# Fixed turn for score banks, one bank for side work, denominators in pairs by transfers and GpSimd, mask kept in memory: one core, masked attention with three layer norms

## The chip, the cores and the metric

The kernel runs on one core of a Trainium2 chip. The metric is device time in microseconds (us), and lower is better. "Slower" or "faster" means a difference of over 2%. TensorE is PE in the profile, VectorE is DVE, ScalarE is ACT, GpSimd is POOL, SyncE is SP.

## The reference, cut to what matters

```python
# x: (F=8, N=2048, C=256) float32; adj: (2048, 2048) int32, about 0.8% ones; H=8 heads, D=32
q, k, v = split(x @ w_qkv)                       # per frame f
scores  = einsum('fnhd,fmhd->fhnm', q, k) / sqrt(D)
attn    = softmax(where(adj > 0, scores, -1e9))
t       = einsum('fhnm,fmhd->fnhd', attn, v)
y       = layernorm(x + t, g1, b1)
z       = layernorm(y + relu(y @ w1 + b1_) @ w2 + b2_, g2, b2)
out     = layernorm(x + z)
```

## The kernel before

A block is 128 keys by 512 queries by four heads. Sixteen blocks are a group (one half of the heads), two groups a chunk of 512 queries, four chunks a frame. For each block PE makes scores into two score tiles (two PSUM banks each), DVE adds the mask while it empties them into a P buffer, ACT takes the exponential in place, and PE multiplies by the values. Two blocks of scores are made ahead.

The softmax denominators are sums of the P buffers over the keys. Seven of sixteen blocks go to PE one by one as products with ones ("lone terms"). Five are added up by GpSimd, four by accumulating transfers, and each of the two sums is one more term:

```python
pp   = pool(bufs=6)                     # P buffers, 1 MB each
ps_s = pool(bufs=3, PSUM)               # three score tiles, also used by all side work
ps_o, ps_d = pool(bufs=1, PSUM), pool(bufs=1, PSUM)     # values' sum, denominator
mask = mkp.tile([P, MB, N], F8)         # the whole mask, on chip
POOLED = (0, 1, 4, 7, 10)
MOVED = (2, 5, 8, 11)
ALONE = [m for m in range(MB) if m not in POOLED + MOVED]
# values(item), after the four value matmuls of block mb:
    if mb == POOLED[1]:
        nc.gpsimd.tensor_tensor(ACC[grp], PT.pop((f, qc, g, POOLED[0])), PT.pop(item), ALU.add)
    elif mb in POOLED[2:]:
        nc.gpsimd.tensor_tensor(ACC[grp], ACC[grp], PT.pop(item), ALU.add)
    elif mb in MOVED[1:]:
        nc.gpsimd.dma_start(PT[f, qc, g, MOVED[0]], PT.pop(item), accum_op=ALU.add)
    terms = [PT.pop(item)] if mb in ALONE else []
    if mb == LAST:
        terms += [ACC.pop(grp), PT.pop((f, qc, g, MOVED[0]))]
    for n, term in enumerate(terms):    # four matmuls each into the denominator's bank
        ...
```

Beside the blocks runs side work, a piece a block: the tail of the chunk before (division, residual, three norms, two layers of the MLP, about 20 blocks long), in the last chunk of a frame the projections of the next frame, and in frame 0 the turning of the mask.

## Time and profile before

| | before |
|---|---|
| time | 4264.85 us median of 3 (4258.01 to 4278.54) |
| profiled run | span 4279.2 us, granted clock 0.954 |
| PE / DVE / ACT / POOL busy | 90 / 66 / 57 / 44% |
| DVE idle in front of a masking, behind scores | 920 us |
| time at half clock, from the clock's records | 392 us |

The prediction shows rows of the page and works out from them what bounds the kernel. Three rows of DVE's waits (columns: us in total, times, longest us):

```profile
DVE p L146 <- PE s L143: 920.2, 676, 24.6
DVE p L146 <- DMA p<-p: 96.9, 59, 3.3
DVE RS L219 <- PE s L217: 100.2, 32, 7.1
```

The second row is DVE waiting for a P buffer that a transfer still reads, the third is the reciprocals waiting for the turned denominators.

### The profile page before, as it was taken

The numbers are of one execution on the slowest core, as the hardware profiler recorded it, in microseconds if no ns is written. First come the engines' busy times: TensorE is split into PE (matmuls) and PEld (weight loads), VectorE is DVE, ScalarE is ACT, GpSimd is POOL, SyncE is SP. The second block draws the span as 40 slices with busy tenths as digits, with TensorE's granted clock in tenths as the row PEclk, the third lists the DMA queues.
The fourth block names the chain that finished last, engine by engine and source line by source line (L and its number), as shares of the span: only waits on it lengthen the run. The fifth ranks groups of instructions, "written<-read, shape, count | busy, mean of one in ns | idle before, by whom it ended". The sixth has DMA issues, their size and how long they took to land. (4 is left out here: it accounts for less than half of the span.)

```text
span 4279.2 us, 57066 instructions
## 1 busy us (share of the span) xinstructions
PE 3863.4 (90%) x24068; PEld 1267.8 (30%) x24068; DVE 2814.4 (66%) x3175; ACT 2439.0 (57%) x1809; POOL 1896.5 (44%) x841
## 2 busy tenths in 40 slices
PE   7988989999999989999899998999989999899996
PEld 3222232222322223222232223322233222332222
DVE  2766747777477765777557775577756777467774
ACT  3655645555466655666555655556655565556564
POOL 1444425545245543545435444355533554344453
PEclk9988999999999999999999999999999999999998
DMA  3342323222233221233223223223231323222222
GB/s 108 73 105 63 69 69 65 55 60 60 60 70 69 60 69 40 60 70 70 69 41 66 62 60 78 41 60 69 61 77 33 69 60 70 69 49 60 60 60 54
DMA packets 89654, 274.13 MB, mean 64 GB/s; under 512 B 6064, under 2 KB 56368, under 8 KB 64816
## 3 DMA queue, kind: packets, MB, share of 16 engines
q0 software_dynamic: 27648, 201.34, 23.4%
q1 hardware_dynamic: 61744, 69.09, 5.2%
q8 instruction: 190, 3.11, 0.3%
q14 instruction: 72, 0.59, 0.0%
HBM read 52.30 MB, written 16.78 MB: 16 GB/s over the span
## 5 line engine op out<-in xcount | busy, mean ns | idle before, releaser
L146 DVE TENSOR_TENSOR p<-s,mask 128x1024 f32<-128x1024 f32 x2048 | 2407.8, 1217 | 1102.6 <-PE s L143 920.2
L148 ACT ACTIVATE p<-p 128x2048 f32<-128x2048 f32 x1024 | 1956.1, 1910 | 1586.5 <-DVE p L146 1264.3
L143 PE MATMUL s<-qT,kT 32*128 32x512 f32 x8192 | 1552.3, 658 | 177.9 <-DVE p L146 164.5
L172 POOL TENSOR_TENSOR acc<-acc,p 128x2048 f32<-128x2048 f32 x192 | 872.7, 4545 | 682.8 <-ACT p L148 525.3
L166 PE MATMUL o<-p,v 128*32 128x512 f32 x8192 | 1137.4, 628 | 35.1 <-ACT oT L185 34.1
L143 PEld LDWEIGHTS s<-qT,kT 32*128 32x128 f32 x8192 | 473.5, 187 | 1119.6 <-DVE p L146 555.7
L181 PE MATMUL den<-p,ones 128*32 128x512 f32 x4096 | 561.3, 621 | 0.0
L170 POOL TENSOR_TENSOR acc<-p 128x2048 f32<-128x2048 f32 x64 | 291.5, 4554 | 474.9 <-ACT p L148 277.6
L166 PEld LDWEIGHTS o<-p,v 128*32 128x32 f32 x8192 | 163.2, 109 | 847.3 <-issue 574.3
L232 POOL TENSOR_TENSOR y<-y,in 128x1024 f32<-128x1024 f32 x32 | 75.4, 2355 | 553.3 <-DVE y L229 553.3
L117 PE MATMUL s<-turned,wqkv 128*128 128x512 f32 x512 | 239.6, 613 | 12.6 <-ACT turned L111 12.6
L181 PEld LDWEIGHTS den<-p,ones 128*32 128x32 f32 x4096 | 140.1, 116 | 341.9 <-issue 340.6
L205 ACT ACTIVATE y<-y,nb,rs 128x256 f32<-128x256 f32 x384 | 198.3, 588 | 45.3 <-DVE nb L203 45.3
L194 DVE BATCH_NORM_STATS2 st<-y 128x6 f32<-128x256 f32 x384 | 154.3, 402 | 73.3 <-POOL y L273 70.9
L197 POOL TENSOR_SCALAR rs<-mv 128x4 f32<-128x4 f32 x96 | 18.2, 190 | 380.4 <-DVE mv L195 377.6
L174 POOL DMA_DIRECT2D p<-p x192 | 170.6, 888 | 27.9 <-ACT p L148 23.5
L117 PEld LDWEIGHTS s<-turned,wqkv 128*128 128x128 f32 x512 | 93.8, 192 | 161.2 <-issue 129.4
L271 POOL TENSOR_TENSOR y<-y,g2r 128x1024 f32<-128x1024 f32 x32 | 76.0, 2376 | 124.3 <-ACT y L205 124.3
L254 PE MATMUL s<-turned,w1s 128*128 128x512 f32 x256 | 121.2, 617 | 3.0 <-ACT turned L246 3.0
L243 PE MATMUL s<-ident,y 128*128 128x128 f32 x256 | 66.0, 349 | 64.0 <-ACT y L205 63.5
L248 POOL TENSOR_TENSOR y<-y,g1r 128x1024 f32<-128x1024 f32 x32 | 75.3, 2352 | 103.3 <-PE s L243 99.8
L264 PE MATMUL s<-w2s,hT 128*128 128x256 f32 x512 | 119.2, 386 | 0.8 <-ACT hT L257 0.8
(55 smaller groups left out, 1683.4 us busy)
## 6 DMA issues: line engine op xcount, KB each, us to landing
p<-p POOLq DMA_DIRECT2D x192, 1024.0 KB, 7.0
in<-in_x_dram SPq DMA_DIRECT2D x64, 512.0 KB, 6.5
in<-in_adj_dram SPq DMA_DIRECT2D x32, 512.0 KB, 5.1
out_dram<-y SPq DMA_DIRECT2D x32, 512.0 KB, 3.3
wqkv<-in_L_gnn_w_qkv_dram SPq DMA_DIRECT2D x1, 768.0 KB, 4.3
w1s<-in_L_gnn_w_dram SPq DMA_DIRECT2D x1, 256.0 KB, 4.5
w2s<-in_L_gnn_w_dram SPq DMA_DIRECT2D x1, 256.0 KB, 4.8
g1r<-in_L_gnn_ln_g_dram SPq DMA_DIRECT2D x1, 128.0 KB, 4.8
```

The lines of the kernel that those rows point to most:

```text
L117: nc.tensor.matmul(ps[:, g, :], wqkv[:, a, k0 + g * P:k0 + (g + 1) * P], xT[:, a, :], start=(a == 0), stop=(a == 1))
L143: nc.tensor.matmul(ps2[half][:, j, :], KT[f, mb // TPC][r:r + D, g, (mb % TPC) * P:(mb % TPC + 1) * P], QT[f, qc][r:r + D, g, :], start=Tr ...
L146: nc.vector.tensor_tensor(pt[:, 2 * half:2 * half + 2, :], ps, mask[:, mb, qc * CH:(qc + 1) * CH][:, None, :].to_broadcast([P, 2, CH]), AL ...
L148: nc.scalar.activation(pt, pt, AF.Exp, scale=1.0 / math.sqrt(D))
L166: nc.tensor.matmul(O[grp][r:r + D, :], V[f, mb // TPC][:, mb % TPC, g * P + r:g * P + r + D], pt[:, h, :], start=(mb == 0), stop=(mb == LAST))
L170: nc.gpsimd.tensor_tensor(ACC[grp], PT.pop((f, qc, g, POOLED[0])), PT.pop(item), ALU.add)
L172: nc.gpsimd.tensor_tensor(ACC[grp], ACC[grp], PT.pop(item), ALU.add)
L174: nc.gpsimd.dma_start(PT[f, qc, g, MOVED[0]], PT.pop(item), accum_op=ALU.add)
L181: nc.tensor.matmul(DEN[grp][r:r + D, :], cst["ones"], term[:, h, :], start=(mb == ALONE[0]), stop=(n == 2))
L194: nc.vector.bn_stats(st, t[:, j, :])
L205: nc.scalar.activation(t[:, j, :], t[:, j, :], AF.Identity, bias=nb[:, j:j + 1], scale=rs[:, j:j + 1])
L254: nc.tensor.matmul(ph[:, d, :], w1s[:, a, d * P:(d + 1) * P], yT[:, a, :], start=(a == 0), stop=(a == 1))
```

## The change

The intent was to take work and waits away from PE and the score banks. Seven pairs of a group are added by accumulating transfers, GpSimd adds up the pairs, and PE gets three terms a group instead of nine, five blocks into the next group. Side work leaves the score tiles: it gets whichever of two single banks the values' sum doesn't use, so the score tiles keep a fixed turn. All of it is cut into smaller pieces, with set numbers of blocks between them. The mask goes to DRAM and 512 queries of it are loaded at a time. The room that this frees makes nine P buffers of six. The residuals come by accumulating transfers straight into y. There is one y buffer.

```diff
-    pp = ctx.enter_context(tc.tile_pool(name="pp", bufs=6))
+    pp = ctx.enter_context(tc.tile_pool(name="pp", bufs=9))
-    ps_s = ctx.enter_context(tc.tile_pool(name="ps_s", bufs=3, space=bass.MemoryType.PSUM))
-    ps_o = ctx.enter_context(tc.tile_pool(name="ps_o", bufs=1, space=bass.MemoryType.PSUM))
-    ps_d = ctx.enter_context(tc.tile_pool(name="ps_d", bufs=1, space=bass.MemoryType.PSUM))
+    ps_s = [ctx.enter_context(tc.tile_pool(name=f"ps_s{i}", bufs=1, space=bass.MemoryType.PSUM)) for i in range(3)]
+    ps_x = [ctx.enter_context(tc.tile_pool(name=f"ps_x{i}", bufs=1, space=bass.MemoryType.PSUM)) for i in range(2)]
... (project, turn_mask, tail: each piece takes one bank() and yields the blocks to wait)
-    POOLED = (0, 1, 4, 7, 10)
-    MOVED = (2, 5, 8, 11)
-    ALONE = [m for m in range(MB) if m not in POOLED + MOVED]
+    NPAIR = MB // 2 - 1
+    ISSUE, ADD, SUM = 2, 5, 20
+    def denominators(t):
+        ...
+        item = block(ISSUE)
+        f, qc, g, mb = item
+        if mb % 2 == 0 and mb // 2 < NPAIR:
+            nc.gpsimd.dma_start(PT[f, qc, g, mb + 1], PT.pop(item), accum_op=ALU.add)
+        f, qc, g, mb = block(ADD)
+        grp, k = (f, qc, g), mb // 2
+        if mb % 2 == 0 and 0 < k < NPAIR:
+            pair = PT.pop((f, qc, g, mb + 1))
+            if k == 1:
+                ACC[grp] = ap.tile([P, 4, CH], F32, name="acc")
+                nc.gpsimd.tensor_tensor(ACC[grp], PT.pop((f, qc, g, 1)), pair, ALU.add)
+            else:
+                nc.gpsimd.tensor_tensor(ACC[grp], ACC[grp], pair, ALU.add)
... (tail)
-        nc.gpsimd.tensor_tensor(y, y, xs, ALU.add)
+        nc.gpsimd.dma_start(y, xin, accum_op=ALU.add)
...
             while (nf, nmb // TPC) not in V:      # a block whose projection isn't made yet
-                advance()
+                advance(t0)                       # runs side work, whatever is first in line
+                t0 += 1
```

## The prediction

> **What bounds the kernel now.** I first read the busy row and the groups of the page. A "block" here is 128 keys by 512 queries by four heads; there are 1024, in 64 groups of 16, two groups to a chunk of 512 queries, 32 chunks.
>
> ```profile
> PE 3863.4 (90%) x24068; PEld 1267.8 (30%) x24068; DVE 2814.4 (66%) x3175; ACT 2439.0 (57%) x1809; POOL 1896.5 (44%) x841
> L146 DVE TENSOR_TENSOR p<-s,mask 128x1024 f32<-128x1024 f32 x2048 | 2407.8, 1217 | 1102.6 <-PE s L143 920.2
> L172 POOL TENSOR_TENSOR acc<-acc,p 128x2048 f32<-128x2048 f32 x192 | 872.7, 4545 | 682.8 <-ACT p L148 525.3
> L181 PE MATMUL den<-p,ones 128*32 128x512 f32 x4096 | 561.3, 621 | 0.0
> L174 POOL DMA_DIRECT2D p<-p x192 | 170.6, 888 | 27.9 <-ACT p L148 23.5
> p<-p POOLq DMA_DIRECT2D x192, 1024.0 KB, 7.0
> ```
>
> PE at 90% looks like the bound, but a matmul that waits for its bank counts as busy. So I went to the timeline of a quiet stretch:
>
> ```profile
> 1999.63 2.36 DVE L146 TENSOR_TENSOR p<-s,mask 128x1024 f32<-128x1024 f32 x2 [0.17 <-PE s L143]
> 2000.44 1.60 PE L143 MATMUL s<-qT,kT 32*128 32x512 f32 x8
> 2001.97 1.07 PE L166 MATMUL o<-p,v 128*32 128x512 f32 x8
> 2002.16 2.36 DVE L146 TENSOR_TENSOR p<-s,mask 128x1024 f32<-128x1024 f32 x2 [0.17 <-PE s L143]
> 2002.85 1.04 PE L181 MATMUL den<-p,ones 128*32 128x512 f32 x8
> 2003.83 1.14 PE L143 MATMUL s<-qT,kT 32*128 32x512 f32 x8
> ```
>
> Two DVE starts lie 2.53 us apart: the first half of the masking frees a bank (1.2), the scores refill it (1.14), about 0.2 of signalling. The scores row shows 1.60 there and 1.14 when nothing is waited for. PE's own work in a plain block is about 2.05 us (scores 1.07 and values 0.97, start to start), so it has 0.48 us of slack; a denominator term of 0.97 us makes the block 2.95, which is 0.42 more. This is a DVE-PE loop and not a full PE.
>
> The starts of the exponentials, read from the timeline, give the chunks: 116.5 us for an ordinary one (1794.94 to 1911.43), 159.7 where the next frame is projected (2064.00 to 2223.70), some 140 for the second and third of frame 0, where masks are turned. 32 plain blocks would take 81.0. The other 35.5 us of an ordinary chunk are, by my reading of the periods: 14 denominator terms at 0.42, 5.9; the two ends of groups, 9.2; the tail (both norms, the MLP, the last norm), about 20.
>
> The tail's long steps are seen here:
>
> ```profile
> 1820.20 0.33 PE L243 MATMUL s<-ident,y 128*128 128x128 f32 x1 [1.52 <-ACT y L205]
> 1825.17 2.36 DVE L146 TENSOR_TENSOR p<-s,mask 128x1024 f32<-128x1024 f32 x2 [4.07 <-PE s L143]
> 1828.00 3.70 PE L254 MATMUL s<-turned,w1s 128*128 128x512 f32 x8
> 1832.91 2.36 DVE L146 TENSOR_TENSOR p<-s,mask 128x1024 f32<-128x1024 f32 x2 [5.38 <-PE s L143]
> 1820.00:1824.00 4.00, 3.60 (x16) 1.95 (x16) 1.10 (x1) 4.00 (x7) 0.83 (x1) 0.57 1.03 209
> 1824.00:1828.00 4.00, 4.00 (x25) 0.60 (x17) 2.36 (x2) 1.14 (x3) 3.92 (x3) 0.58 0.28 57
> ```
>
> DVE sits idle for 4 to 5 us behind one piece of side work on PE. The last two rows are windows (length, busy of PE, PEld, DVE, ACT, POOL, granted clock, DMA): after PE's 1.5 us wait the clock is 0.57 for 8 us.
>
> **What the skill says.** "SBUF — State Buffer", section "SBUF: two separate sides": GpSimd and a VectorE operation with two SBUF inputs take the shared ports as an exclusive lock, for the whole instruction. The trace agrees: the small nb (both inputs in SBUF) takes 151 ns free and a median of 1274, at most 4264, and those over 1 us that I looked at end some 20 ns after a GpSimd addition. The masking reads one operand from PSUM and keeps 1217 ns beside GpSimd or not. "TensorE: Matmul & The Clock Gate", section "What's actually happening", has the array fall to half clock after an idle window; the windows above agree in kind. "DMA: Bandwidth & Descriptors", section "Anatomy of one DMA — SWDGE (gpsimd) path", gives about 2.0 us plus bytes over 436 GB/s, an estimate of 4.4 us for 1 MB. This trace has 7.0 for the accumulating transfer, which I use.
>
> **The change part by part.**
>
> Denominators. Nine terms a group become three: seven pairs are added by transfers, GpSimd sums the seven, and PE takes the sum and the last two blocks, five blocks into the next group. PE busy falls by two thirds of 637 us (561.3 and 76.2 for the acc form), 425 us, but most of that lay in slack. On the path, before: 5.9 + 9.2 = 15.1 us a chunk. After: two steps of 3 x 0.97 = 2.9, less slack 0.48, so 2.4 each, and about 0.5 each for turning and the reciprocal: 5.9. Saving 9.2 a chunk.
>
> Banks. Side work no longer takes a score bank, so the turn of three pairs is kept and a score waits for one half of a masking. Before, a step with side work shifted the turn, so that both halves had to be masked first: 3.66 to 3.78 us even when PE's piece was small, 1.2 lost. But side work now has one bank, and consecutive pieces wait for its emptying behind the exponential: masking 2.4, exponential 1.95, copy 0.75, then scores and piece; two blocks share about 6.4 us plus the piece f, so a block takes (6.4 + f)/2: 4.1 for f = 1.87, 3.7 for f = 1.0. The tail then costs: two normalising steps 0.65 each, three statistics 2.0 each, three nb 1.25 each, two turns 3.2 in all, four MLP pieces 1.6, 1.6, 1.4, 1.4, a collision with the denominator 1.3, about 22. The same as before within my error; I credit 1 us.
>
> Projection. Per 512 rows two turns and six pieces of 1.9 us, at 0.9 and 1.6 beyond a plain block: 11.4, four times 46 a frame, against 43 now. A loss of 3 a frame. Masks of frame 0: eight small PE steps at 1.1 and eight DVE steps at 0.85, 15 against 23 a chunk, three times: 24 less in all.
>
> GpSimd. 384 additions at 4.55, 448 issues at 0.888, 128 tail operations at 2.37, 117 of rs, 64 issues for the residuals: 1747 + 398 + 303 + 117 + 57 = 2622 us, 65% of 4010. In a plain run it needs 5.4 us for two blocks that take 5.06, so it falls behind in a group and catches up at its end. The accumulating transfers go from 23.4% to 54.6% of the engines' time, 5.2 us each (1001 us over 192), again more than two blocks.
>
> New waits. z's residual is now a transfer after two GpSimd operations: from the norm's end 4.7 + 0.9 + 7 to 8 us, against about 11 us of blocks before the statistics need it, so some 2.5 us of DVE waiting. The two operations also delay the additions behind them, and with them the p buffers, by up to 4 to 5 us. y's transfer may cost 1.5. Together 0 to 9 us a chunk; nine p buffers absorb part: I take 4.
>
> Sum. 9.2 + 1 - 4 = 6.2 a chunk, times 32: 198. Projection +21 (seven frames), masks -24, the end +8 (two transfers and two group sums in a row where nothing covers them). 4265 - 198 + 21 - 24 + 8 = 4072. The mean clock of 0.954 means about 9% of the span at half speed, some 390 us, where up to 195 us can be lost; no 3.7 us piece and a shorter wait should save a third, 62. That gives **4010 us**.
>
> **Rivals.** (1) GpSimd becomes the bound: its order is strict, an issue stands behind an addition, the addition behind a landing. For it: 5.4 against 5.06 us. Against it: only 14 of 16 blocks load it and it is at 65% on average. It would eat the saving: 4150 to 4300. (2) The denominators were all hidden in slack and side work stays additive: then only the ends of groups gain, 4150. (3) The fixed turn matters more than I credit, because DVE's 920 us idle behind scores are mostly its doing, and the nine buffers hold: half of those gone gives 3750 to 3850.
>
> **Range and chances.** Rivals 1 and 3 pull by some 200 us each way, so 3820 to 4190. The line of 2% is 4180, near the top of that: faster 0.85, same 0.12, slower 0.03. The staggering looks fitted to these latencies, which is part of why I do not go lower in chance.
>
> **What would show it.** Denominator matmuls at about 210 us busy; idle of DVE behind scores well under 920; ordinary chunks near 110; GpSimd near 2600 busy; granted clock above 0.954. Wrong if DVE's maskings wait for transfers or GpSimd over 300 us in all (97 on transfers now), if the denominators wait for acc on PE, if nb grows beyond 2.5 us, or if the statistics wait for the y transfers by more than 4 us each.

## The result, and the profile after

The changed kernel took 4561.93 us (median of 4, 4557.8 to 4589.01) against 4263.87 us before (the three runs above and one more). The ratio is 1.0707, 95% interval 1.0657 to 1.0757: slower by 7%. A ratio is the mean time of one kernel's fast runs over that of the other's of the same rounds, so it isn't quite the ratio of the medians. The output is correct.

The page of the kernel after, its busy row, groups (busy us, mean ns of one, idle before it and what ended most of it) and one row of its transfers:

```profile
PE 3456.5 (76%) x20996; PEld 1038.2 (23%) x20996; DVE 2881.5 (63%) x3207; ACT 2458.0 (54%) x1953; POOL 2640.3 (58%) x1227
L180 DVE TENSOR_TENSOR p<-s,mask 128x1024 f32<-128x1024 f32 x2048 | 2409.2, 1218 | 1217.2 <-PE s L177 814.6
L220 POOL TENSOR_TENSOR acc<-acc,p 128x2048 f32<-128x2048 f32 x320 | 1523.0, 4759 | 238.2 <-DMA p<-p 231.9
L235 DVE SCALAR_TENSOR_TENSOR nb<-mv,rs 128x4 f32<-128x4 f32 x96 | 141.5, 1474 | 14.3 <-POOL rs L232 14.3
L250 PE MATMUL x<-p,ones 128*32 128x512 f32 x1024 | 129.3, 625 | 25.9 <-ACT turned L295 13.5
p<-p POOLq DMA_DIRECT2D x448, 1024.0 KB, 7.6
```

PE has less to do, and DVE and ACT are busy for a smaller share than before; GpSimd went from 44 to 58%. No engine has become full. The additions (L220) now wait for transfers, 232 us. Rows of DVE's waits in the kernel after:

```profile
DVE p L180 <- PE s L177: 814.6, 486, 19.2
DVE y L280 <- DMA out_dram<-y: 176.7, 30, 8.7
DVE p L180 <- issue: 133.1, 170, 6.8
DVE p L180 <- ACT hT L304: 112.2, 35, 3.3
DVE st L227 <- DMA y<-in_x_dram: 88.1, 17, 13.3
DVE p L180 <- POOL acc L220: 50.1, 33, 3.1
DVE p L180 <- DMA p<-p: 31.1, 21, 3.3
DVE rc L260 <- PE x L256: 24.7, 6, 16.9
```

The row "issue" belongs to the wait behind scores, for those gaps end some 0.1 us after a score matmul has. So do most of the rows that name ACT. Here is one of the 35 that name hT:

```profile
1514.15 1.98 PE L303 MATMUL x<-turned,w1s 128*128 128x512 f32 x4 [1.58 <-ACT turned L295]
1516.07 1.14 PE L177 MATMUL s<-qT,kT 32*128 32x512 f32 x8
1516.17 0.69 ACT L304 ACTIVATE hT<-x,b1s 128x512 f32<-128x512 f32 x1
1517.33 2.35 DVE L180 TENSOR_TENSOR p<-s,mask 128x1024 f32<-128x1024 f32 x2 [3.26 <-ACT hT L304]
```

hT had ended 0.47 us before the masking began, the scores 0.12. They stood on PE behind a piece of the MLP, which itself had waited 1.58 us for ACT. By the semaphore that changed last, 151 of the 179 us in front of maskings that the profile puts down to ACT ended with scores. Counted so, with "issue" and ACT's rows, maskings waited 1135 us for scores, where it was 1002.

New are the wait of y's first product for the store of the y before (5.9 us each, 30 times) and the statistics behind the residual's transfer. The reciprocals wait less than before, 25 us for 100.

A quiet stretch of the timeline of the kernel after:

```profile
1869.31 2.35 DVE L180 TENSOR_TENSOR p<-s,mask 128x1024 f32<-128x1024 f32 x2 [0.20 <-PE s L177]
1870.59 1.14 PE L177 MATMUL s<-qT,kT 32*128 32x512 f32 x8 [0.42 <-DVE p L180]
1871.86 2.35 DVE L180 TENSOR_TENSOR p<-s,mask 128x1024 f32<-128x1024 f32 x2 [0.19 <-issue]
```

A plain block takes 2.55 us, where it took 2.53. Here PE now waits visibly (0.42 us) where it used to have a lone term to work on or a queued matmul that counted as busy. So a plain block gained nothing, and could not: its loop is masking, scores, signalling.

A change of frame in the kernel after:

```profile
1731.98 2.35 DVE L180 TENSOR_TENSOR p<-s,mask 128x1024 f32<-128x1024 f32 x2
1738.94 0.69 DVE L280 TENSOR_TENSOR y<-x,rc 128x512 f32<-128x512 f32 x1 [4.61 <-DMA out_dram<-y]
1743.38 3.78 PE L145 MATMUL x<-turned,wqkv 128*128 128x512 f32 x4 [0.68 <-ACT turned L138]
1747.98 0.43 DVE L227 BATCH_NORM_STATS2 st<-y 128x6 f32<-128x256 f32 x1 [6.45 <-DMA y<-in_x_dram]
1758.57 1.98 PE L145 MATMUL x<-turned,wqkv 128*128 128x512 f32 x4 [0.68 <-ACT qT L147]
1767.03 2.36 DVE L180 TENSOR_TENSOR p<-s,mask 128x1024 f32<-128x1024 f32 x2 [15.23 <-PE s L177]
```

The next block needs a projection that hasn't been made, so the loop that forces side work runs pieces of the tail and of the projection one after another, with both y waits in it. No masking starts for some 34 us. The same piece of four matmuls takes 3.78 us there at half clock and 1.98 at full clock.

Mean lengths of the chunks, from starts of exponentials, frames 1 to 6 (two runs are listed for later):

| chunk of the frame | before | after | denominators alone | those without transfers | after without transfers |
|---|---|---|---|---|---|
| first | 124.7 | 165.8 | 132.5 | 127.2 | 169.4 |
| second | 117.5 | 121.3 | 120.5 | 113.0 | 110.6 |
| third | 117.6 | 128.9 | 123.2 | 112.8 | 114.5 |
| last (projections) | 159.7 | 139.5 | 161.6 | 153.8 | 126.2 |
| frame | 519.5 | 555.5 | 537.8 | 506.8 | 520.7 |

The changed kernel gains 20 us in a frame's last chunk and loses 41 in the first, but it also loses 4 and 11 in the two ordinary ones. From the start of the last exponential to the end it is 91.9 us, where it was 58.0.

### The profile page after: what moved, and what is told of

Read it like the earlier page. It is cut to its first block, busy times and chain, and to the rows that moved or that the text cites. A ratio compares the mean times of both kernels' runs of the same rounds, so it can differ in the third digit from the quotient of the medians.

```text
span 4556.7 us, 51690 instructions
## 1 busy us (share of the span) xinstructions
PE 3456.5 (76%) x20996; PEld 1038.2 (23%) x20996; DVE 2881.5 (63%) x3207; ACT 2458.0 (54%) x1953; POOL 2640.3 (58%) x1227
## 5 line engine op out<-in xcount | busy, mean ns | idle before, releaser
L177 PE MATMUL s<-qT,kT 32*128 32x512 f32 x8192 | 1301.0, 708 | 511.8 <-DVE p L180 511.4
L220 POOL TENSOR_TENSOR acc<-acc,p 128x2048 f32<-128x2048 f32 x320 | 1523.0, 4759 | 238.2 <-DMA p<-p 231.9
L194 PE MATMUL x<-p,v 128*32 128x512 f32 x8192 | 1203.6, 663 | 14.8 <-ACT p L182 11.5
L211 POOL DMA_DIRECT2D p<-p x448 | 445.8, 1005 | 1020.7 <-PE x L194 866.4
L194 PEld LDWEIGHTS x<-p,v 128*32 128x32 f32 x8192 | 167.2, 112 | 898.7 <-issue 649.4
L145 PE MATMUL x<-turned,wqkv 128*128 128x512 f32 x480 | 267.2, 685 | 92.1 <-ACT kT L147 50.1
L227 DVE BATCH_NORM_STATS2 st<-y 128x6 f32<-128x256 f32 x384 | 153.8, 401 | 88.1 <-DMA y<-in_x_dram 88.1
L303 PE MATMUL x<-turned,w1s 128*128 128x512 f32 x256 | 130.6, 633 | 47.8 <-DVE rc L260 24.8
L235 DVE SCALAR_TENSOR_TENSOR nb<-mv,rs 128x4 f32<-128x4 f32 x96 | 141.5, 1474 | 14.3 <-POOL rs L232 14.3
L250 PE MATMUL x<-p,ones 128*32 128x512 f32 x1024 | 129.3, 625 | 25.9 <-ACT turned L295 13.5
L312 PE MATMUL x<-w2s,hT 128*128 128x256 f32 x512 | 127.6, 392 | 3.6 <-DVE rc L260 1.1
```

The lines of the kernel that those rows point to most:

```text
L145: nc.tensor.matmul(ps, wqkv[:, a, k0 + g * P:k0 + (g + 1) * P], xT[:, a, :], start=(a == 0), stop=(a == 1))
L177: nc.tensor.matmul(ps2[half][:, j, :], KT[f, mb // TPC][r:r + D, g, (mb % TPC) * P:(mb % TPC + 1) * P], QT[f, qc][r:r + D, g, :], start=Tr ...
L194: nc.tensor.matmul(O[grp][r:r + D, :], V[f, mb // TPC][:, mb % TPC, g * P + r:g * P + r + D], PT[item][:, h, :], start=(mb == 0), stop=(mb ...
L211: nc.gpsimd.dma_start(PT[f, qc, g, mb + 1], PT.pop(item), accum_op=ALU.add)
L220: nc.gpsimd.tensor_tensor(ACC[grp], ACC[grp], pair, ALU.add)
L227: nc.vector.bn_stats(st, t[:, j, :])
```

## The experiments

Every run has the time of the kernel before beside it on the same chip (medians 4264 to 4270 us).

| run | edit | us | ratio to before (95%) | clock |
|---|---|---|---|---|
| e1 | after, two y buffers | 4505.81 | 1.0552 (1.0523 to 1.058) | 0.902 |
| e2 | after, forced loop runs projections alone | 4600.48 | 1.0781 (1.0754 to 1.0808) | 0.899 |
| e3 | after, constant matmuls in idle blocks | 4586.38 | 1.0739 (1.0699 to 1.0778) | 0.916 |
| e4 | before, no lone terms (wrong) | 4174.47 | 0.9773 (0.9743 to 0.9803) | 0.932 |
| e5 | before with the new denominators alone | 4433.88 | 1.0382 (1.0365 to 1.04) | 0.906 |
| e6 | before with the mask in memory alone | 4273.18 | 1.001 (0.9994 to 1.0027) | 0.958 |
| e7 | before, no projections after frame 0 (wrong) | 3914.53 | 0.9169 (0.9152 to 0.9185) | 0.962 |
| e8 | after, no projections after frame 0 (wrong) | 4240.85 | 0.9927 (0.9904 to 0.9949) | 0.881 |
| e9 | e6 with nine P buffers, three loading buffers | 4202.67 | 0.9863 (0.9845 to 0.9881) | 0.961 |
| e10 | e5 with constant matmuls in place of the removed terms | 4565.06 | 1.0699 (1.0667 to 1.0732) | 0.919 |
| e11 | e5 without its transfers (wrong) | 4172.7 | 0.9795 (0.9766 to 0.9824) | 0.929 |
| e12 | e5 without its additions (wrong) | 4168.31 | 0.9773 (0.9756 to 0.9789) | 0.921 |
| e13 | after without its pair transfers (wrong) | 4284.66 | 1.004 (1.0019 to 1.006) | 0.931 |
| e14 | after without its additions (wrong) | 4294.85 | 1.0068 (1.0039 to 1.0097) | 0.926 |
| e15 | e9 with two lone terms of seven moved | 4282.34 | 1.0018 (0.9989 to 1.0047) | 0.945 |
| e16 | e1 with the residual loaded and added by GpSimd | 4392.48 | 1.0285 (1.0265 to 1.0306) | 0.917 |
| e17 | e5, transfers one block earlier | 4390.9 | 1.0301 (1.0274 to 1.0327) | 0.901 |
| e18 | e5, additions two blocks later | 4462.12 | 1.0457 (1.0426 to 1.0488) | 0.895 |

I began with the theories that the trace suggested: new waits of the tail (y, its store, its transfers), the clock that falls because PE has too little to do, and the forced projections.

**e1, two y buffers.**

```diff
+    yp = ctx.enter_context(tc.tile_pool(name="yp", bufs=2))
-        y = work.tile([P, TPC, C], F32, name="y")
+        y = yp.tile([P, TPC, C], F32, name="y")
```

> The changed kernel with two buffers for y, so that the next tail's first product need not wait for the store of the last output. In its profile VectorE is idle 176.7 us for that store (30 times). Theory W (the loss is the new waits): that idle time goes to under 20 us and the time falls by 150 to 260 us, to about 4350. Theory C (the loss is TensorE's clock, which falls because little is left to do in a window): the idle time goes, but the time at half clock stays near 900 us and the time falls by less than 100 us. Rival: the wait is only moved, as the single chain of the tail fills the chunk anyway: then within 40 us of 4562.

It gained 56 us. The store wait is gone, and in DVE's waits the statistics took up much of it:

```profile
DVE st L228 <- DMA y<-in_x_dram: 173.6, 29, 13.8
```

That row was 88.1 us. The wait moved in part from the store to the transfer behind it. Theory C's numbers fit too: the time at half clock stayed at 885 us. This run doesn't tell the two apart.

**e2, projections alone in the forced loop.**

```diff
-                advance(t0)
+                force(t0)      # takes the projection first; the tail only if that is what it waits for
```

> The changed kernel, but where a block can't start before its projection, only the projection is run to its end; the tail no longer is pulled through in the same place. In the changed kernel's profile one such place lasts about 36 us (no block in it), at 7 frame changes. Theory W: the first chunk of a frame falls from 163 to about 145 us, in all 100 to 130 us less, about 4445. Theory C: the same direction but half of that, since the projection by itself still stops the blocks for about 20 us at half clock.

It got slower by 38 us, and the first chunk stayed long, at 168. The projections had to be made then in either case, and the tail was late afterwards. So the order in the forced loop isn't the cause; that the work is left over at that point is.

**e3, keeping PE busy.** Four matmuls of constants, 224 columns each, in the free bank, in blocks in which PE had no side work in this step or the one before.

```diff
+            keep_warm()        # for h in range(4): matmul(ps[32h:32h+32, 0:224], ones, wqkv[:, 0, 0:224])
```

> The changed kernel with work added: in blocks without side work on TensorE, four matmuls of constants (224 columns, about 0.43 us of the array) into the free side bank, read by nothing, just before the scores, where TensorE waits 0.41 us anyway. Theory C: the share of time at half clock falls from 20% (mean clock 0.898) to 12% or less (0.94), and the kernel gets faster by 60 to 200 us although it does more. Theory W: no gain, 0 to 60 us slower, as the added work pushes the scores a little.

The clock rose by 0.018 and the time by 24 us. Work added in quiet blocks doesn't reach the long waits in which the clock falls, and it costs its own time.

**e4, the lone terms taken out of the kernel before.** The result is wrong; this is the most that taking them off PE can be worth there.

```diff
-        for n, term in enumerate(terms):
+        for n, term in enumerate(terms if mb == LAST else []):
```

> The kernel before, with the matmuls of the denominators left out in all blocks but the last of each group, and nothing else changed (the denominators are wrong on purpose; seven alone terms less one, 6 of 9). By my prediction's sum a term costs 0.42 us on the path: 12 terms a chunk, 32 chunks, 161 us less, 4103. Theory C: TensorE's busy share in many windows falls under a half, the mean clock falls from 0.954 to 0.93 or less, and of the 161 us at most 80 are gained; the time is 4185 or more.

Removing them for nothing gains 96 us, where the sum of the prediction's slack gives 12 terms at 0.42 us in 32 chunks, 161. The time at half clock rose from 392 to 571 us. PE now idles in part of their place, and some of the gain may go to the slower clock. That is argued from the two numbers and not tested by itself.

**e5, the new denominators alone.** Mask in memory, nine P buffers, pairs by transfers and GpSimd at the same distances as in the changed kernel, three terms a group; the old banks, tail and residual.

```diff
-    POOLED = (0, 1, 4, 7, 10) ... terms, as above
+    the denominators(t) of the change, with ps_d.tile for the three terms
```

> The kernel before with one part of the change: mask in memory (for the room), nine p buffers, pairs added by transfers and summed by GpSimd, three denominator terms five blocks into the next group. Score banks, side work, tail and the loads of the residual as before. My prediction's sum for this part alone: 9.2 us a chunk saved, less up to 4 for waits on p buffers: 4100 to 4000. Theory C (clock): the same 425 us of matmuls go away, the mean clock falls to 0.93 or less and half of it is lost: 4110 to 4200. Theory P (the transfers and GpSimd's strict order are what makes the changed kernel slow): 4265 or more, with VectorE's maskings waiting over 150 us for transfers and GpSimd.

This part alone makes the kernel 164 us slower. Of GpSimd and DVE in that run (first two rows: DVE's, then GpSimd's waits):

```profile
DVE p L156 <- DMA p<-p: 179.5, 73, 6.1
DVE p L156 <- POOL acc L195: 96.2, 79, 2.3
...
POOL acc L195 <- DMA p<-p: 231.3, 120, 9.0
POOL acc L193 <- DMA p<-p: 131.3, 32, 6.8
```

Maskings wait 276 us for P buffers, which transfers and additions still hold. GpSimd stands 363 us in additions that wait for a transfer, with the issue of the next transfer behind them on its queue.

**e6, the mask in memory alone.** (The mask tile per 512 queries, a store after it is turned, a load per chunk; six P buffers.)

```diff
-    mask = mkp.tile([P, MB, N], F8, name="mask")
+    MD = dp.tile([NCK, P, MB, CH], F8, name="md")
+        nc.sync.dma_start(MK[f, qc], MD[qc])
```

> The kernel before with the mask kept in memory per 512 queries and loaded for each chunk, nothing else (six p buffers, five load buffers). All theories: within 15 us of before; theory P would allow 20 to 40 us more from 28 more transfers of 1 MB.

No effect. Its use is the room.

**e7 and e8, no projections after frame 0**, in the kernel before and in the changed one. All frames use frame 0's, so both results are wrong.

```diff
-                fill.append(project(f + 1, ...))
+    QT, KT, V of all frames = those of frame 0
```

> The kernel before, all frames using the projections of frame 0 (outputs of frames 1 to 7 wrong on purpose). By the chunks of the profile, 7 x 49 us less: 3920.

> The changed kernel, likewise without projections. By the chunks of its profile, 7 x (165 + 140 - 2 x 124) = 400 us less: 4160. Theory F (the frame changes are what makes the changed kernel slower than before): the distance between these two kernels shrinks from 297 us to under 100. Theory O (ordinary chunks are slower: waits of the tail, clock): it stays at 170 us or more.

Without projections the two kernels are 326 us apart, with them 298. So the projections, which look worst in the timeline, don't make the difference: without them each chunk of the changed kernel is some 10 us longer (127 against 117).

**e9, what the freed room is worth.** The kernel before with e6's mask and nine P buffers.

```diff
-    ld = ... bufs=5      pp = ... bufs=6
+    ld = ... bufs=3      pp = ... bufs=9
```

> The kernel before with the mask kept in memory (which alone moved nothing) and nine P buffers in place of six, paid for with two loading buffers fewer (three in place of five). Nothing else of the change. In the kernel before the maskings waited 97 us for transfers between P buffers. If P buffers are what limits such a kernel, those 97 us mostly go: 4180 to 4220. If the wait only stood where the wait for the scores would have stood, as the first prediction holds for most of the waits, 4250 to 4270. If three loading buffers are too few, over 4280.

It gained 63 us over the kernel before. The waits for P buffers are no longer among DVE's waits, and those behind scores did not rise (873.0 and, under "issue", 61.1, against 920.2 and 23.4). This run is correct and under both kernels: 1.4% under before, clear of noise but within the 2% that counts as the same.

**e10, the clock.** The denominators alone, with the removed matmuls put back on constants.

```diff
+        if mb in (3, 6, 9, 12, 13, 14):
+            for h in range(4): matmul(dm[32h:32h+32, :], ones, wqkv[:, 0, 0:512])
```

> The denominators alone (the run that came to 4434 us) with the six removed terms of a group put back as matmuls of constants with the same shape at the blocks where the kernel before has them, results unused: PE has again the work of before, and the transfers, the additions and the waits of the new order stay. Theory clock (the removed matmuls had kept the array at full speed; half-clock time 841 us here against 392 before): the time falls under 4400 and the granted clock goes back to about 0.94. Theory waits (transfers and additions in strict order hold the P buffers, the array's clock only follows): the time rises by 30 to 100 us, to 4460 to 4530, since PE work is only added; the clock may rise nonetheless.

It got slower by 131 us, though the clock rose from 0.906 to 0.919. So the missing matmuls aren't what makes e5 slow. The terms cost more here than in the kernel before (131 against 96 us).

**e11 and e12, half of the pair chain each.** The even block of a pair is dropped instead of transferred; or a constant tile takes the place of the sum.

```diff
-            nc.gpsimd.dma_start(PT[f, qc, g, mb + 1], PT.pop(item), accum_op=ALU.add)
+            PT.pop(item)                          # e11
-                nc.gpsimd.tensor_tensor(ACC[grp], ACC[grp], pair, ALU.add)
+            ACC[grp] = fixed                      # e12, a tile of ones
```

> The denominators alone without their 448 transfers (the even block of a pair is dropped, so the result is wrong on purpose); the additions on GpSimd stay, at the same blocks. If the transfers cost the 164 us (the P buffer held for 7.5 us more, additions that wait for them 363 us, DVE waiting 180 us on them), the time comes down to 4200 to 4270. If the additions do, by what they share with DVE, it stays over 4380. Between these, both.

> The denominators alone without the additions on GpSimd (a constant tile of ones takes the place of the sum, wrong on purpose); the 448 transfers stay. If the additions cost the 164 us (DVE's small operations that wait while GpSimd adds: the nb products took 1535 ns each here against 1082 before; the P buffers held until an addition has ended, 96 us), the time comes down to 4200 to 4300. If the transfers do, it stays over 4380. With transfers started earlier (GpSimd's queue is free), P buffers come free earlier in any case, worth up to 50 us.

Either alone takes away 261 or 266 us and lands at e4's time. So neither the transfers alone nor the additions alone cost much there. It is having both, one behind the other. (No run leaves both out; e4, with the old sums and six buffers, is the nearest to it.) Against e9, which has the nine buffers alone, e11 and e12 are only some 30 us faster: with nine buffers that is what the removed terms are still worth. The nb product (both inputs in SBUF) measures what the additions share with DVE. The nb group of e5:

```profile
L224 DVE SCALAR_TENSOR_TENSOR nb<-mv,rs 128x4 f32<-128x4 f32 x96 | 147.3, 1535 | 4.3 <-POOL rs L219 4.3
```

and of e12:

```profile
L224 DVE SCALAR_TENSOR_TENSOR nb<-mv,rs 128x4 f32<-128x4 f32 x96 | 14.7, 153 | 4.3 <-POOL rs L219 4.3
```

The sharing costs 133 us of DVE, but e11, which has the additions and 92.8 us in nb, is as fast as e12, which has neither. So the sharing doesn't account for the 261 us.

**e13 and e14, the same two cuts in the changed kernel** (same edits).

> The changed kernel without its 448 transfers between P buffers (the even block of each pair is dropped, wrong on purpose); additions, banks, tail and everything else as changed. With the old banks and tail the same removal took the denominators alone from 4434 to 4173, 261 us. If the pair chain does the same damage in the changed kernel, the time falls from 4562 by 200 to 300, to 4260 to 4360, and what is left over 4173 (90 to 190 us) belongs to the banks and the tail. If with the new banks and tail another chain ends last (y's store, one bank for side work, maskings waiting for P buffers only 81 us here against 276), it falls by less than 120 us and stays over 4440.

> The changed kernel without the additions on GpSimd (a constant tile in their place, wrong on purpose), the 448 transfers kept. Same two theories as for the run without transfers: 4260 to 4360 if the pair chain is what costs here too; over 4440 if the banks and the tail end last. If the time falls here but not without the transfers, it is what the additions share with DVE (nb products 1474 ns each) and not the order on GpSimd's queue.

They take away 277 and 267 us. The pair chain costs in the changed kernel what it costs alone, although there the maskings wait only 81 us for P buffers: its price shows up as other waits. Without transfers DVE's waits in front of maskings fall by 150 us, and the waits of y's products from 248 to 142 (sums of DVE's idle stretches over 0.1 us, as all such sums here). What is left over e11, 112 us, belongs to the banks and the tail. The second chunk is now 110.6 us, against 113.0 in e11, but the third is 114.5 against 112.8: ordinary chunks come out about even. The last chunk gains 28 us, the first loses 42, and 28 more are lost after the last exponential (84.9 against 56.7).

**e15, an attempt to go below e9.**

```diff
-    POOLED = (0, 1, 4, 7, 10)         MOVED = (2, 5, 8, 11)
+    POOLED = (0, 1, 4, 7, 10, 11)     MOVED = (2, 3, 6, 9, 12)
```

> A try at a version that beats both: the kernel before with the mask in memory and nine P buffers (4203 us), and two lone denominator terms of seven a group moved: one more block by a transfer into the moved sum (blocks 2, 3, 6, 9, 12), one more by an addition (0, 1, 4, 7, 10, 11). No lone term at all is worth 4174 with six buffers, and 4170 or so with nine, so at most 35 us are to be had; two of seven terms: 4185 to 4200 if GpSimd, with 26 of 40 us a group then, keeps up. If the order on GpSimd's queue costs as with the pairs, 4210 to 4300.

One transfer and one addition more in a group cost 80 us, though they take two terms from PE. A miss, and its cause isn't separated: no masking waits for a P buffer there and no addition for a transfer; PE's denominators wait 47 us for the moved sum, and nb rose from 106 to 148 us.

**e16, the tail's transfers.** Two y buffers, and the residual loaded into a buffer of its own and added by GpSimd (one loading buffer fewer pays for it).

```diff
+        xs = xp.tile([P, TPC, C], F32, name="xs")
+        nc.sync.dma_start(xs, xin)
-        nc.gpsimd.dma_start(y, xin, accum_op=ALU.add)
+        nc.gpsimd.tensor_tensor(y, y, xs, ALU.add)
```

> The changed kernel with two y buffers (which alone gave 4506 us, with the statistics then waiting 174 us for y's accumulating transfers), and the residual brought by a load into a buffer of its own and added by GpSimd, as in the kernel before, in place of the two accumulating transfers a tail; one loading buffer less pays for it. If these waits are what the tail adds, 4400 to 4460. If GpSimd's queue (another 64 additions of 2.4 us, 152 us in all) is what ends last, no gain: 4490 to 4560.

It gained 113 us over e1 and 169 over the changed kernel, although GpSimd has 64 additions more. DVE's waits before it writes y fell from 248 to 71 us and those before the statistics from 88 to 54. So with the pair chain in place the single y and its two accumulating transfers cost 169 us, and GpSimd isn't short of time. The first chunk still takes 160 us, so this isn't what was left over in e13; and as the residual's transfers stood on the queue of the pair chain, part of the 169 may be the chain's. No run has both taken out.

**e17 and e18, which part of the chain.** The distances in blocks from a pair to its transfer and to its addition:

```diff
-    ISSUE, ADD, SUM = 2, 5, 20
+    ISSUE, ADD, SUM = 1, 5, 20     # e17
+    ISSUE, ADD, SUM = 2, 7, 20     # e18
```

> The denominators alone (4434 us) with the transfers one block earlier (issued one block after their even block, not two), the additions where they were: four blocks, 10 us, from issue to addition instead of three, 7.6 us, against 7.5 us from issue to landing. In the run at 4434 GpSimd stood 363 us in its additions waiting for transfers, with the next transfer behind them on the same queue. If that strict order is what costs, most of these waits go and the time falls by 50 to 150 us, to 4280 to 4380. If it is GpSimd's own time (an issue of 0.9 to 1.2 and an addition of 4.65 to 4.84 us a pair are 5.6 to 6.0 in two blocks of 5.06) and what the two share, nothing changes: 4410 to 4450.

> The denominators alone with the additions two blocks later (seven blocks behind, not five), the transfers where they were: the additions hardly wait for transfers any more, but every finished pair holds its P buffer two blocks longer, and nine buffers are then just enough. If the strict order on the queue is what costs, the time falls, to 4300 to 4400. If the P buffers are (maskings waited 276 us for them), it rises, to 4500 to 4650.

Neither expectation fits e17: it gained 43 us. The groups of e17 show that the additions have stopped waiting for transfers:

```profile
L195 POOL TENSOR_TENSOR acc<-acc,p 128x2048 f32<-128x2048 f32 x320 | 1543.1, 4822 | 7.8 <-DMA p<-p 5.1
```

That takes these waits out almost wholly (363 us became 5) and the waits for P buffers fell from 276 to 74 us, but five sixths of the 261 us stay. The queue keeps its order, though: an issue that waits for PE still stands in front of an addition. In e18 the additions hardly wait either (22 us), the buffers are held two blocks longer (286 us of waiting for them), and it loses 28. My sum of 5.6 to 6.0 us a pair in the expectation counted an overlap twice: an addition starts some 0.6 us after the issue, so a pair takes about 5.5. In e17 GpSimd stands idle 894 us behind PE before its issues, so its pace isn't the bound there either.

Where DVE's time went, from the traces in us:

| | before | e11 | e5 | e17 | after | e13 |
|---|---|---|---|---|---|---|
| span | 4279 | 4164 | 4440 | 4363 | 4557 | 4276 |
| maskings wait for scores ("issue" and ACT's rows included) | 1002 | 1049 | 948 | 1118 | 1135 | 1065 |
| maskings wait for P buffers | 97 | 0 | 276 | 74 | 81 | 1 |
| nb products | 104 | 93 | 147 | 103 | 142 | 141 |
| writes of y (products, MLP's sum) wait | 94 | 86 | 86 | 87 | 248 | 142 |
| reciprocals wait | 100 | 81 | 91 | 89 | 25 | 18 |
| statistics wait | 73 | 36 | 34 | 47 | 88 | 65 |
| time at half clock | 392 | 597 | 841 | 867 | 927 | 590 |

In the first row the profile puts 59, 0, 218, 153, 179 and 20 us down to ACT; by the semaphore that changed last 6, 0, 5, 20, 28 and 20 are really ACT's. From e11 to e17 the waits for P buffers give 74 of 199 us, and those for scores 69. (These are the profiled runs; e17's was the fastest of its four, which lie from 4365 to 4408, and by the medians it is 218.) That PE stood 270 us longer at half clock, in which at most half is lost, would fit the latter. No run separates it, and what remains of the chain's cost in e17 stays open. More than nine P buffers with the chain in place were not tried.

## Why the prediction was wrong

It said 4010 us, 255 less than before; it came to 298 more. The readings of the profile held: the DVE-PE loop of 2.5 us, the 200 us of denominator matmuls left (129.3 and 69.3), GpSimd's 2622 us (2640.3). The sum failed in these terms:

1. **"Saving 9.2 a chunk"** (294 us). Taking all the lone terms away for nothing is worth 96 us, 3.0 a chunk (e4). e11 and e12, which move the ends of groups as well and have nine buffers, gain no more (93 and 97 us). The prediction counted each term's 0.42 us and the groups' ends as if nothing took their place. What did isn't shown; in e4 the time at half clock rose by 179 us.
2. **"it falls behind in a group and catches up at its end"** (of GpSimd). This is the step that failed by its reading. Outside the rivals it is all that the prediction has on transfer and addition in a row, and in the sum it costs nothing. The pair chain costs 261 us alone and 267 to 277 in the changed kernel, 8 a chunk (e5 against e11 and e12; after against e13 and e14). That 8 lies within "together 0 to 9 us a chunk" is luck: that term (128 us as taken) was made of z's residual, y's transfer and the operations before them. Rival 1 named the chain ("an issue stands behind an addition, the addition behind a landing") but took GpSimd for the bound, set it aside for GpSimd's average of 65%, and would have let it eat the saving only. The average is no argument: GpSimd is at 58% and not the bound, either half of the chain alone is close to free (measured against e4), and both in a row cost 6%. e17 shows that the additions' waits for transfers are about a sixth of it. The rest stays open.
3. **"I credit 1 us" for the banks, projection +21, masks -24, the end +8** (27 us less in all). The banks and the tail cost 112 to 128 us (e13 against e11, after against e5). The prediction credited neither the first chunk (42 us longer, with projections left over that are then made in a row) nor y's store: it held "z's residual ... some 2.5 us" and "y's transfer may cost 1.5", while in the changed kernel the waits for y's store and for its transfer came to 5.9 and 5.2 us a time, and the end cost 28 (34 with the chain) instead of 8. e16 gets 169 us back by two y buffers and plain loads, with the chain in place. Without the chain the ordinary chunks come out about even, which is near the credit of 1.
4. **"A shorter wait should save a third, 62" of the half-clock time.** It rose from 392 to 927 us. With idle gaps where matmuls had been, PE falls to half clock more often. It was no lever to pull, though: filling blocks with matmuls of constants raised the clock and made the changed kernel and e5 slower (e3, e10).

Put together: -96 for the terms, +261 for the chain, +128 for banks and tail is +293, against +298 measured. This is no check of the parts: it goes from before over e4's or e11's time and e5 to after, so it must come out. And the parts overlap: in e11 the nine buffers are in the gain for the terms, and e16 gets back more than the 128. The mask in memory is worth nothing by itself (e6), as the prediction assumed by leaving it out, and the buffers that it pays for were worth 63 in the kernel before (e9).

The signs that I listed didn't all help. Maskings waited 81 us for transfers and GpSimd, not over 300, and nb's mean was 1.47 us, not over 2.5, and yet the time was off. The chain's price had turned into longer waits elsewhere. The signs that did answer were the chunks (121 and 129, not 110), DVE's idle time behind scores (not under 920 with "issue" counted), the clock, the denominators, which did wait for acc on PE (40 us in all, none before), and the statistics' wait (5.2 us each where it occurred).

## What to carry to other kernels

Price a chain of asynchronous steps by taking out each link once: here a transfer and an addition that each cost next to nothing cost 6% in a row, and in the changed kernel neither the engines' averages nor the direct wait rows showed it. Before moving hidden work off an engine, take it out for nothing (a wrong result is fine): here that bounded the gain at 96 us, and the buffers that the change made room for gave 63 of gain without any of the rest. A wait that the profile puts down to one engine may have ended with another: look at what ended last before it. And before merging two buffers into one, count what must land between one use and the next: the single y waited 177 us for its store.

## What the Trainium skill lacked or had wrong

- "TensorE: Matmul & The Clock Gate", section "What's actually happening", says when the array is slow (after an idle window of 3413 ns), not how idle the window must be. Under "A second HAM failure mode: psum-queue depth-cycling" it lets short idle gaps do it, without a number. I cut the traces into windows of 3413 ns on the grid of the clock's changes. In the kernel after, all 131 windows at full clock in which PE was busy for under 40% were followed by half clock, and of 870 over 55% none was; in between it went both ways. Under 40% always meant half clock in the traces of before, e5, e11, e13 and e17 too, but the upper figure doesn't carry over: in e5 35 windows of 55 to 75% were followed by half clock (busy includes waiting for a bank). A window with gaps in it is enough; it need not be idle (in the stretch that the prediction shows, PE had waited 1.5 us).
- "DMA: Bandwidth & Descriptors", section "Anatomy of one DMA — SWDGE (gpsimd) path", gives one fit for this path, an estimate of 4.4 us for 1 MB from its numbers. Accumulating transfers of 1 MB between buffers on the chip landed in 7.0 us in the kernel before and 7.6 in the one after. The page has no time for accumulating ones.
- "SBUF — State Buffer", section "SBUF: two separate sides", on the shared ports: the runs agree (nb products 1535 ns on average beside GpSimd's additions, 153 without). What it can't say is that these 133 us don't account for the loss.
- No page that I read says what an accumulating transfer and an engine's addition cost when one waits for the other on one queue (261 us here, next to none for either alone). The profile's time of an addition right behind a transfer's issue is longer (4889 ns on average for the 316 of them in e17, against 4539 for the other 68), but it starts some 0.27 us before the issue has ended, so most of that is overlap.
